# Four pre-LN graph layers on one core: kept blocks copied ahead of a row's weights, new planning numbers, and a new end

## The chip, the cores and the metric

One core of a Trainium2 chip runs the whole program. Five engines work side by side: TensorE (PE) multiplies, VectorE (DVE) and ScalarE (ACT) do elementwise work, GpSimd (POOL) does a little of both, and SyncE (SP) issues most of the transfers. The metric is the time of one launch on the device, in microseconds (us); the median of three runs is given.

## The reference

Sixteen graphs (batches) of 1,024 nodes with 128 features pass through four layers. Each layer adds its result to x; all of them use the same dense 1024 x 1024 adjacency `adj`, symmetric in its pattern, not in its values.

```python
h = relu(layernorm(x)); x = x + L0(h, adj)      # and so for L1, L2, L3
# L0: three times (relu after the first two)
h = h @ W + b
nh = h / max(norm(h), EPS)
h = (adj * (nh @ nh.T)) @ h
# L1
y = relu(((1 + eps) * h + adj.T @ h) @ W1 + b1) @ W2 + b2     # zero where masked
# L2: attention of one head
h = h @ W
attn = softmax(where(adj > 0, tanh(h @ a[:f] + (h @ a[f:]).T), -1e15))
y = where(sum(adj, 1) == 0, x, attn @ h)
# L3
h = x @ Ww.T + Wb
e = (h @ A) @ h.T;  e = e + e.T
att = softmax(where(adj > 0, e, 0), axis=1) * adj
hp = relu(att @ h)
i, f, o = sigmoid([x, hp] @ gate weights + biases)
y = o * tanh(sigmoid(i * hp + f * x))
```

## The kernel before

**Tiling.** A batch's x is one tile of 128 partitions by eight blocks of 128 columns: node 128c + p lies on partition p, block c. A 1024 x 1024 matrix is worked on in eight rows j of 128, each row in two halves s of 512 columns (four blocks). A half fills one PSUM bank.

**adj.** `turn` loads each row of the transposed adjacency in squares of 32 by 32, four transfers to a tile (L724, on SP), turns the squares on DVE (L732), and sums rows on ACT (L735). Batch b + 1's tiles are loaded while batch b runs.

**Layer 0.** Each of three sublayers (named 00, 01, 02) projects h (PE, L461), adds the bias and scales (L505 where the scale is the last sublayer's norm), flips h into hTn (PE transposes L451, ACT copies L483), sums squares on ACT and DVE (L770, L776), and raises them to −1/2 on GpSimd (`rn`, L444). Then for every row j: `square.row` fills the two halves of the row of h hT in PSUM (`sq`), `ew` on DVE multiplies it with rn and adj (L791), and PE accumulates with it (L671 or L682).

**The symmetric square.** h hT is symmetric, so `Square` multiplies only the blocks on and above the diagonal (L609). The blocks above the diagonal are kept in an SBUF tile `above`, and a later row transposes them back into its bank with PE (`mirrored`, L619). `keep` writes them: a copy on ACT (L641), behind L791 in the program, from the bank that L791 reads. A bank of PSUM is read by one engine after the other: the planner makes every operation on a bank wait for the one before it if that is on another engine. In batches 1 to 13 (`FAR`) the lower left quarter takes another way: DVE transposes rows 0 to 3's right halves (L631), SP sends them to HBM and fetches them back as squares (L651, L662), and DVE reads them in SBUF (`got`). Layer 3 uses the same class with e = g hT, where g is arranged to make it symmetric.

**Layers 1 to 3.** Layer 1 accumulates over adj rows loaded plainly (`adjL`) and runs two small matmuls (L471, L844). Layer 2 makes scores on ACT (tanh L906, exp L910), masks them on DVE (L914), and accumulates on PE (L682). Layer 3, for a row: mask (L973, reading the square's bank), row maximum (L984), exp on ACT (L988), times adj in two halves on DVE (L995), a scale of h's row by the sum (`hs`, L1004), accumulation (L671). Its end: hpT (L483), a projection `psN` (L461), hp (L1017), three gates for each node (add L1029, tanh L1035, scale L1038), z = hn * gate on GpSimd (L1043), z = hp * gate + z on DVE (eight instructions of 128 x 128, L505), two tanh on ACT (L1049, L1050), z = z * gate + x on DVE (again eight, L505), and the output's transfer (L1056, issued on ACT's queue).

**The order of work.** No engine chooses at run time: each works through its instructions as they were written. A list scheduler, `Plan`, writes them. Every operation has a planned duration, its predecessors and its buffers. At each step the planner takes the operations that could start next, and among those that can start within `WINDOW` of the earliest on the same engine it takes the one with the lowest rank: the batch's due time (`b * PERIOD`, and `(B - 2) * PERIOD + LAST` for the last), less the work behind it, less a lead from the table `LEADS` for this kind of operation (the key is layer, engine and buffer). `POOLS` gives how many buffers of a kind there are and `KINDS` how many a use may hold, with a smaller share for later batches. So work of up to three batches stands mixed in each engine's queue.

Of the kernel before, what the change touches and what calls it, by code (L numbers as in the profile page):

```python
# [53 lines left out]
class Plan:  # L54
# [53 lines left out]
    def link(self):  # L108

        for o in self.ops:
            for b in [b for b in o.new if b.kind == "ps"]:
                for r in b.users:
                    if r is not o:
                        for t in [t for t in r.new if t.kind not in self.psum]:
                            r.new.remove(t)
                            o.new.append(t)
        behind = {o: set(o.preds) for o in self.ops}
        for o in self.ops:  # L120
            for b in o.new:
                for u in b.users:
                    if u is not o:
                        self.place_after(u, o)
                        behind[u].add(o)
        for o in self.ops:
            for b in [b for b in o.new if b.kind in self.psum]:
                for u in b.users:
                    for p in behind[u]:
                        if p.seq < o.seq:  # L130
                            self.place_after(o, p)
        for o in reversed(self.ops):
            o.tail = o.us + max((s.tail + o.lat for s in o.succs), default=0.0)
            o.rank = (self.deadline(o.batch) - o.tail - self.leads.get(o.key, 0.0), o.seq)
# [87 lines left out]
def tile_adj_preln(  # L222
# [97 lines left out]
    for load_it in first:  # L320
# [11 lines left out]
    POOLS = {"adjT": 16, "adjL": 5, "x": 3, "big": 13, "above": 2, "got": 1, "bank": 8, "small": 24, "row": 5, "hbm": 3}  # L332
    KINDS = {
        "adjT": ("adjT", 16, 16), "adjL": ("adjL", 5, 5), "x": ("x", 3, 3), "w4": ("big", 9, 8),
        "chunk": ("big", 10, 4), "above": ("above", 2, 1), "got": ("got", 1, 1), "ps": ("bank", 4, 4),
        "acc": ("bank", 8, 5), "small": ("small", 16, 6), "row": ("row", 5, 5), "hbm": ("hbm", 3, 2),
    }
    PERIOD, LAST, AHEAD, WINDOW = 66.0, 23.0, 2, 0.05

    LEADS = {  # L340
        "0 ACT hT": 3.5, "0 ACT hn": 18.5, "0 DVE hn": 14.5, "0 DVE nb": -43.5, "0 DVE st": -4, "0 PE ps": 13.5,
        "0 POOL rstd": -24, "00 ACT above": 74, "00 ACT hTn": -86, "00 ACT params": -0.5, "00 ACT sq": 49,
        "00 DMA by": 16.5, "00 DMA got": 16.5, "00 DVE above": -7.5, "00 DVE ew": 1, "00 DVE h": -224.5,
        "00 DVE params": 64.5, "00 DVE ss": 12.5, "00 PE acc0": -62, "00 PE ps": 81.5, "00 PE psP": 523.5,
        "00 PE sq": -15, "00 POOL rn": -26.5, "01 ACT above": 69, "01 ACT hT": 19, "01 ACT hTn": -158,
        "01 ACT sq": 4.5, "01 DMA by": 18.5, "01 DMA got": 31, "01 DVE above": 1.5, "01 DVE ew": 316.5,
        "01 DVE h": 20, "01 PE ps": 12, "01 PE psP": 27, "01 PE sq": 55.5, "01 POOL rn": 19, "02 ACT above": -1,
        "02 ACT hTn": -32, "02 ACT sq": -30.5, "02 DMA by": 21, "02 DVE above": -1, "02 DVE ew": -53.5,
        "02 DVE h": 3, "02 DVE ss": -403, "02 DVE x": -30, "02 PE acc0": -29.5, "02 PE ps": -131.5,
        "02 PE psP": 13, "02 PE sq": -24.5, "02 POOL rn": 20, "1 DMA adjL": -497, "1 DVE adjL": 4.5,  # L350
        "1 DVE hn": 238, "1 DVE mv": 35.5, "1 DVE nb": -17, "1 DVE st": -449, "1 DVE x": -3.5,
        "1 PE acc1": -32.5, "1 PE py": -31.5, "1 PE py2": -32, "1 POOL rstd": -28, "2 ACT e2": -33.5,
        "2 ACT h": 2, "2 ACT hfl": -64, "2 ACT hn": -370, "2 ACT hnT": -5.5, "2 ACT s1": 1.5,
        "2 DVE alone": -36, "2 DVE e2": 5.5, "2 DVE h": -125.5, "2 DVE hn": 74.5, "2 DVE hrow": 5,
        "2 DVE mv": 60, "2 DVE nb": 263.5, "2 DVE rden": 23, "2 DVE st": 153, "2 DVE x": 18.5, "2 PE p1": -18,
        "2 PE pf": -240.5, "2 PE ps": -21, "2 PE psP": -186, "2 POOL rstd": -12.5, "3 ACT above": -206,
        "3 ACT e3": -111.5, "3 ACT gT": -84, "3 ACT gate": 81.5, "3 ACT h3T": -30.5, "3 ACT hn": -79,
        "3 ACT hnT": 243, "3 ACT hp": -80.5, "3 ACT hpT": 102.5, "3 ACT hs": -38.5, "3 ACT z": -290.5,
        "3 DMA by": 49, "3 DMA z": 1.5, "3 DVE e3": -89, "3 DVE gate": 68.5, "3 DVE h": -14.5, "3 DVE hn": 4.5,
        "3 DVE nb": -41, "3 DVE st": -5.5, "3 DVE sum": -15.5, "3 DVE z": -618, "3 PE acc3": -42.5,  # L360
        "3 PE pg": -27, "3 PE ps": 23, "3 PE psN": -301.5, "3 PE psP": -25, "3 PE sq": -17.5,
        "3 POOL rstd": -23.5, "3 POOL z": 3.5, "T DMA adjT": -143, "T DVE adjT": -223.5, "x DMA x": -51,
# [4 lines left out]
    def op(engine, us, reads, writes, fn, port=False, lat=None):  # L367
        o = plan.op(engine, us, reads, writes, fn, now[0], port, lat)
        t = (list(writes) + list(reads))[0]
        o.key = f"{now[1]} {engine} {(t[0] if isinstance(t, tuple) else t).name.split('_')[0]}"  # L370
        return o
# [4 lines left out]
    def act(us, reads, writes, fn):  # L376
        return op("ACT", us, reads, writes, fn)

    def dve(us, reads, writes, fn, port=False):
        return op("DVE", us, reads, writes, fn, port)  # L380
# [27 lines left out]
    FAR = range(1, B - 2)  # L408
# [37 lines left out]
    def flip(src, lo, hi, dst, w=D):  # L446
# [6 lines left out]
        pe((hi - lo) * TR, [blk(src, lo, hi, w)], [dst], emit)  # L453

# [59 lines left out]

    def layernorm(k, xt, behind=None):
# [47 lines left out]

        lo, hi = HALVES[0]
# [5 lines left out]
    def relu(t):  # L570

        lo, hi = HALVES[0]
# [120 lines left out]
    def load(b):  # L693
        xt = Buf("x", [P, N], f"x_{b}")
        op(
            "DMA", 2.2, [], [xt],
            lambda: nc.sync.dma_start(by_block(xt.t), x[b].rearrange("(c p) d -> p c d", p=P)),
        )
# [41 lines left out]
    def layer0(b, xt, aT, prepared):  # L740
        now[1] = "0"
        hn = layernorm(f"{b}_0", xt)
        hT = flipped(hn, f"hT_{b}_0", AF.Relu)
        rn = None
        for i in range(3):
# [18 lines left out]
            hTn = flipped(h, f"hTn_{k}")  # L764
            ss = small(f"ss_{k}", NB)
            sq = w4(f"sq_{k}")
            for lo, hi in HALVES:
# [15 lines left out]
            square = Square(k, hTn, hTn, b in FAR)  # L783
            acc = [bank(f"acc0_{k}_{s}") for s in range(2)]
            for j in range(NB):
                ew = chunk(f"ew_{k}_{j}")
                for s, (lo, hi) in enumerate(HALVES):
                    pc, view = square.row(j, s)
                    o = dve(
# [7 lines left out]
                    square.keep(j, s, pc)  # L797
# [15 lines left out]
    def layer1(b, xt, prepared):  # L813
# [6 lines left out]
        add_scaled(xt, D, 0, NB, b12, 0, 0, maskT, m, xt, True)  # L820
# [30 lines left out]
    def layer2(b, xt, aT, su):  # L851
# [10 lines left out]
        add_scaled(xt, D, 0, NB, hn, 0, D, alone, 0, xt, True)  # L862
# [25 lines left out]
        s1 = w4(f"s1_{b}")  # L888
        for s, (lo, hi) in enumerate(HALVES):
            p1 = ps(f"p1_{b}_{s}")  # L890
# [50 lines left out]
    def layer3(b, xt, aT):  # L941
# [3 lines left out]
        hnT = flipped(hn, f"hnT_{k}", AF.Relu)  # L945
        relu(hn)
        gT = w4(f"gT_{b}")
        for s, (lo, hi) in enumerate(HALVES):
            p = ps(f"pg_{b}_{s}")
            wide(p, wg, hnT, lo, hi)  # L950
            evict(p, gT, lo, hi, AF.Identity, bg)
# [12 lines left out]
        hT = flipped(h, f"h3T_{b}", w=E3)  # L964
        square = Square(k, gT, hT, b in FAR)
        acc = [bank(f"acc3_{b}_{s}") for s in range(2)]
        for j in range(NB):
            e = chunk(f"e3_{b}_{j}")
            for s, (lo, hi) in enumerate(HALVES):
                p, view = square.row(j, s)  # L970
                dve(
# [7 lines left out]
                square.keep(j, s, p)  # L979
# [12 lines left out]
            for lo, hi in HALVES:  # L992
# [29 lines left out]
        gate = small(f"gate_{b}", 3 * NB)  # L1022

        def of(g, n=NB):
            return gate.t.rearrange("p (g c) -> p g c", g=3)[:, g, :]

        dve(
            TINY, [hp, h], [gate],
            lambda: nc.vector.tensor_add(  # L1029
                gate.t.rearrange("p (g c) -> p c g", g=3),  # L1030
                by_block(hp.t, E3)[:, :, D:], by_block(h.t, E3)[:, :, D:],
            ),
            True,
        )
        act(0.22, [gate], [gate], lambda: nc.scalar.activation(gate.t, gate.t, AF.Tanh, scale=0.5))  # L1035
        dve(
            TINY, [gate], [gate],
            lambda: nc.vector.tensor_scalar(gate.t, gate.t, 0.5, 0.5, op0=ALU.mult, op1=ALU.add), True,  # L1038
        )
        z = w4(f"z_{b}")  # L1040
        pool_op(
            1.9, [hn, gate], [z],
            lambda: nc.gpsimd.tensor_mul(by_block(z.t), by_block(hn.t), per_node(of(1))),  # L1043
        )
        add_scaled(z, D, 0, NB, hp, 0, E3, gate, 0, z, True)

        def squash():
            v = z.t[:, 0:N]
            nc.scalar.activation(v, v, AF.Tanh, scale=0.5)  # L1049
            nc.scalar.activation(v, v, AF.Tanh, scale=0.5, bias=half)  # L1050

        act(S(N) + S(N, True), [z], [z], squash)
        add_scaled(z, D, 0, NB, z, 0, D, gate, 2 * NB, xt, True)
        op(
            "DMA", 2.0, [z], [],
            lambda: nc.scalar.dma_start(out[b].rearrange("(c p) d -> p c d", p=P), by_block(z.t)),  # L1056
        )
# [77 lines left out]
    with tc.manual_schedule():  # L1135
        for o in ordered:
            for t in o.new:
                src = psum if t.kind in plan.psum else hbm if t.kind == "hbm" else pool
# [36 lines left out]
```

## Time and profile before

| | us |
|---|---|
| median of three runs (2484.53 to 2487.31) | 2484.54 |
| the profiled execution | 2483.96 |
| its span, first to last instruction | 2481.8 |
| PE busy | 2410.6 |
| DVE busy | 2119.4 |
| ACT busy | 1287.1 |
| POOL busy | 214.4 |
| transfers | 263.35 MB, 106 GB/s |

A profile line for a group of instructions gives the kernel's line, engine, operation, the tiles written and read, the shapes and the count; then busy us and the mean ns of one; then the engine's idle time just before these instructions, with what ended most of it. In a list of instructions the columns are start, length, and then the same; square brackets hold the idle time before and its releaser. A list of stretches gives the length, the busy time of each engine with the instructions in brackets, the granted TensorE clock (1.00 is full), the share of time in which the transfer engines worked, and GB/s. Matmul ends are modelled, so the spacing of starts says more than busy time.

### The profile page before, as it was taken

To read this page: it belongs to the slowest core of one execution; us is meant where nothing else is said; L and a number is where in the kernel's file an instruction comes from. 1 tells how busy PE (TensorE), PEld (TensorE's weight loads), DVE (VectorE), ACT (ScalarE), POOL (GpSimd) and SP (SyncE) were. 2 spreads that over 40 slices of the span, in tenths; PEclk is the share of its full clock that TensorE was granted. 3 is DMA by queue.
4 is the path that set the end of the run, shared out by engine and by line. 5 is a ranking of instruction groups with operands and counts; after the bars stand their busy time and mean duration, and the time that the engine had idled before them with its cause. 6 is when DMAs were issued, how large, how long until landed. Compare 5 with 4: busy or idle time off the path is not lost.

```text
span 2481.8 us, 34726 instructions
## 1 busy us (share of the span) xinstructions
PE 2410.6 (97%) x11946; PEld 1588.7 (64%) x11946; DVE 2119.4 (85%) x5278; ACT 1287.1 (52%) x2401; POOL 214.4 (9%) x134
## 2 busy tenths in 40 slices
PE   6999999999999999999999999999999999999987
PEld 3567566675766657566675766756566575765763
DVE  6767989898897989889898897988989899796777
ACT  4425554644646455454554636456454655554575
POOL 1000010010101011011010100101011010010100
PEclk9999999999999999999999999999999999999998
DMA  7622827648284563936648276473945638054100
GB/s 125 129 67 69 163 59 143 138 80 167 60 160 121 99 140 84 165 91 127 129 94 178 52 154 135 84 154 68 165 107 111 136 85 162 1 108 80 35 1 18
DMA packets 1129441, 263.35 MB, mean 106 GB/s; under 512 B 971824, under 2 KB 1112880, under 8 KB 1129264
## 3 DMA queue, kind: packets, MB, share of 16 engines
q1 hardware_dynamic: 1108352, 251.73, 50.0%
q10 hardware_dynamic: 20912, 9.40, 1.4%
q8 instruction: 94, 1.54, 0.3%
q14 instruction: 83, 0.68, 0.1%
HBM read 198.14 MB, written 62.91 MB: 105 GB/s over the span
## 4 chain that ended last, share of the span: by engine, by line
PE 78%; DVE 9%; ACT 7%; issue 2%; DMA 1%; SPq 1%; ACTq 0%; POOL 0%; POOLq 0%; DVEq 0%
PE acc L671 31%; PE sq L609 17%; PE acc L682 11%; PE psP L461 6%; PE sq L619 4%; ACT e L906 3%; DVE ew L791 3%; ACT e L910 3%; PE py L844 2%; PE py L471 2%; DVE e L914 2%; PE ps_hTn L451 1%; DVE z L505 1%; PE pg L471 1%; PE ps_hnT L451 1%
## 5 line engine op out<-in xcount | busy, mean ns | idle before, releaser
L791 DVE SCALAR_TENSOR_TENSOR ew<-sq,rn,adjT 128x512 f32<-128x512 f32 x612 | 436.9, 739 | 68.2 <-PE sq L619 32.0
L671 PE MATMUL acc<-ew,h 128*128 128x512 f32 x1024 | 480.6, 597 | 4.7 <-DVE ew L791 4.5
L609 PE MATMUL sq<-hTn 128*128 128x512 f32 (+3 forms) x1152 | 441.3, 489 | 0.4 <-ACT hTn L483 0.4
L641 ACT COPY above<-sq 128x384 f32<-128x384 f32 (+3 forms) x432 | 169.2, 394 | 403.9 <-DVE ew L791 366.5
L671 PEld LDWEIGHTS acc<-ew,h 128*128 128x128 f32 x1024 | 178.9, 191 | 174.0 <-issue 112.9
L609 PEld LDWEIGHTS sq<-hTn 128*128 128x128 f32 x1152 | 193.5, 191 | 124.0 <-issue 76.1
L682 PEld LDWEIGHTS acc<-h,e 128*128 128x128 f32 x2048 | 241.0, 192 | 29.3 <-DVE e L914 11.8
L682 PEld LDWEIGHTS acc<-h,ew 128*128 128x128 f32 x2048 | 240.8, 192 | 21.0 <-DVE ew L791 11.4
L444 POOL TENSOR_TENSOR rstd<-ve,mhalf 128x8 f32<-128x8 f32 x64 | 104.8, 1637 | 1725.7 <-DVE ve L536 1694.9
L682 PE MATMUL acc<-h,ew 128*128 128x128 f32 x2048 | 252.7, 276 | 0.4 <-DVE ew L791 0.4
L682 PE MATMUL acc<-h,e 128*128 128x129 f32 x2048 | 249.5, 277 | 2.8 <-DVE e L914 1.5
L671 PE MATMUL acc<-e,hs 128*128 128x512 f32 x512 | 240.6, 595 | 1.7 <-DVE e L995 1.7
L671 PE MATMUL acc<-adjL,hn 128*128 128x512 f32 x512 | 239.0, 595 | 0.1
L988 ACT ACTIVATE e<-e,top 128x1024 f32<-128x1024 f32 x128 | 147.1, 1149 | 173.0 <-DVE top L984 172.5
L735 ACT ACTIVATE adjT<-adjT 128x1024 f32<-128x1024 f32 x128 | 135.0, 1055 | 194.0 <-DVE adjT L732 163.7
L619 PEld LDWEIGHTS sq<-ident,above 128*128 128x128 f32 x960 | 125.7, 141 | 142.2 <-issue 74.0
L619 PE MATMUL sq<-ident,above 128*128 128x128 f32 x960 | 174.4, 275 | 27.8 <-ACT above L641 27.8
L914 DVE SCALAR_TENSOR_TENSOR e<-adjT,e 128x512 f32<-128x512 f32 x256 | 162.0, 683 | 41.9 <-ACT e L910 41.9
L732 DVE STREAM_TRANSPOSE adjT<-adjT 128x1024 f32<-128x1024 f32 x128 | 155.2, 1225 | 17.8 <-DMA adjT<-in_adj_dram 10.9
L995 DVE TENSOR_TENSOR e<-e,adjT 128x512 f32<-128x512 f32 x256 | 166.2, 680 | 0.0
L906 ACT ACTIVATE e<-s,h 128x1024 f32<-128x1024 f32 x128 | 143.1, 1141 | 38.4 <-issue 36.6
L631 DVE STREAM_TRANSPOSE above<-sq 128x512 f32<-128x512 f32 x208 | 147.0, 707 | 10.5 <-PE sq L609 9.1
(124 smaller groups left out, 3455.9 us busy)
## 6 DMA issues: line engine op xcount, KB each, us to landing
adjT<-in_adj_dram SPq DMA_DIRECT2D x512, 128.0 KB, 3.7
adjL<-in_adj_dram SPq DMA_DIRECT2D x128, 512.0 KB, 4.9
by_hbm<-above SPq DMA_DIRECT2D x104, 512.0 KB, 3.2
got<-by_hbm SPq DMA_DIRECT2D x416, 128.0 KB, 3.0
x<-in_x_dram SPq DMA_DIRECT2D x16, 512.0 KB, 5.3
out_dram<-z ACTq DMA_DIRECT2D x16, 512.0 KB, 3.3
b<-in_L_gnn_b_dram ACTq DMA_DIRECT2D x4, 64.0 KB, 3.8
w<-in_L_gnn_W_dram ACTq DMA_DIRECT2D x2, 128.0 KB, 3.8
```

The lines of the kernel that those rows point to most:

```text
L461: nc.tensor.matmul(dst.t[:, (c - lo) * n : (c - lo + 1) * n], cols(srcT.t, c), w, start=True, stop=True)
L609: lambda: nc.tensor.matmul(dst.t[:, (first - lo) * P :], cols(leftT.t, j), span(rightT.t, first, hi), start=True, stop=True),
L619: nc.tensor.transpose(cols(dst.t, r), cols(above.t, p), ident)
L641: lambda: nc.scalar.copy(span(above.t, p, p + hi - first), read.t[:, (first - lo) * P :]),
L671: lambda s=s, lo=lo, hi=hi: nc.tensor.matmul(acc[s].t, cols(h.t, at, w), span(ew.t, lo, hi), start=(j == 0), stop=(j == NB - 1)),
L682: nc.tensor.matmul(a.t[:, (c - lo) * n : (c - lo + 1) * n], cols(ew.t, c), h.t[:, j * w : j * w + n], start=(j == 0 and c == lo), stop=(j ...
L732: dve(V(N), [t], [t], lambda t=t: nc.vector.transpose(t.t, t.t), True)
L791: lambda view=view, ew=ew, rn=rn, j=j, lo=lo, hi=hi: nc.vector.scalar_tensor_tensor(by_block(span(ew.t, lo, hi), D, 4), view(), rn.t[:, j ...
L906: lambda e=e, j=j: nc.scalar.activation(e.t[:, 0:N], s1.t[:, 0:N], AF.Tanh, bias=h.t[:, j * E2 + D + 1 : j * E2 + D + 2]),
L914: lambda e=e, j=j, lo=lo, hi=hi: nc.vector.scalar_tensor_tensor(span(e.t, lo, hi), span(aT[j].t, lo, hi), 0.0, span(e.t, lo, hi), op0=ALU. ...
L988: lambda e=e, top=top, tot=tot: nc.scalar.activation(e.t[:, 0:N], e.t[:, 0:N], AF.Exp, bias=top.t, accum_out=tot.t),
L995: lambda e=e, j=j, lo=lo, hi=hi: nc.vector.tensor_mul(span(e.t, lo, hi), span(e.t, lo, hi), span(aT[j].t, lo, hi)),
```

## The change

Five things are changed in the program, each under a letter in a set `FLAGS`; other letters of the set keep what the kernel had, and branches of letters not in the set issue nothing.

- **k**: `square.keep` stands ahead of the operation that weights a half row (L791 and L973), so ACT's copy of kept blocks, or DVE's transposition of them, is written before the weight on the same bank.
- **x**: batch 0's x is loaded by two transfers of half its blocks.
- **z**: in the last two batches, the odd rows of layer 3 are multiplied with adj on GpSimd, in one instruction of 128 x 1024, in place of two on DVE (L995).
- **y**: in the last two batches, z = hp * gate + z and z = z * gate + x are each a multiplication and an addition on GpSimd, in place of eight instructions on DVE (L505).
- **h**: the last batch's end, from the gates to the output's transfer, is done for four blocks and then for the other four. For this the gates of one node lie side by side (c g) where they were by kind (g c).

The planner gets other numbers: ACT's operations 0.03 us longer, DVE's 0.015; own leads for the first two and last two batches (keys that end in <0, <1, >1, >0), some 400 of them; all other leads new; PERIOD, LAST, and the limits on buffers new. What order it then writes follows from all of these.

```diff
-            o.rank = (self.deadline(o.batch) - o.tail - self.leads.get(o.key, 0.0), o.seq)
+            lead = self.leads.get(o.key + o.edge, self.leads.get(o.key, 0.0))
+            o.rank = (self.deadline(o.batch) - o.tail - lead, o.seq)
...
-    POOLS = {"adjT": 16, "adjL": 5, "x": 3, "big": 13, "above": 2, "got": 1, "bank": 8, "small": 24, "row": 5, "hbm": 3}
+    POOLS = {"adjT": 16, "adjL": 5, "x": 3, "big": 13, "above": 2, "got": 1, "bank": 8, "small": 29, "row": 8, "hbm": 3, "hrow": 2}
     KINDS = {
-        "adjT": ("adjT", 16, 16), "adjL": ("adjL", 5, 5), "x": ("x", 3, 3), "w4": ("big", 9, 8),
-        "chunk": ("big", 10, 4), "above": ("above", 2, 1), "got": ("got", 1, 1), "ps": ("bank", 4, 4),
-        "acc": ("bank", 8, 5), "small": ("small", 16, 6), "row": ("row", 5, 5), "hbm": ("hbm", 3, 2),
+        "adjT": ("adjT", 16, 16), "adjL": ("adjL", 5, 5), "x": ("x", 3, 3), "w4": ("big", 10, 6),
+        "chunk": ("big", 12, 4), "above": ("above", 2, 1), "got": ("got", 1, 1), "ps": ("bank", 8, 8),
+        "acc": ("bank", 8, 8), "small": ("small", 7, 6), "row": ("row", 4, 2), "hbm": ("hbm", 3, 2),
+        "hrow": ("hrow", 2, 1),
     }
-    PERIOD, LAST, AHEAD, WINDOW = 66.0, 23.0, 2, 0.05
+    PERIOD, LAST, AHEAD, WINDOW = 60.0, 9.0, 2, 0.05
...
+        o.edge = f" <{now[0]}" if now[0] < 2 else f" >{B - 1 - now[0]}" if now[0] > B - 3 else ""
...
-        return op("ACT", us, reads, writes, fn)
+        return op("ACT", us + 0.03, reads, writes, fn)
...
-        return op("DVE", us, reads, writes, fn, port)
+        return op("DVE", us + 0.015, reads, writes, fn, port)
...
-    FAR = range(1, B - 2)
+    FLAGS = set("Cabcdkxhyz")
+
+    LO, HI = 1, 2
...
+        for lo, hi in HALVES if "x" in FLAGS and b == 0 else ((0, NB),):
+            op(
+                "DMA", 2.2 * (hi - lo) / NB, [], [blk(xt, lo, hi)],
...
-            square = Square(k, hTn, hTn, b in FAR)
+            square = Square(k, hTn, hTn, "abc"[i] in FLAGS and LO <= b < B - HI)
...
                     pc, view = square.row(j, s)
+                    if "k" in FLAGS:
+                        square.keep(j, s, pc)
                     o = dve(
                         V(HALF, True), [pc, rn, blk(aT[j], lo, hi)], [blk(ew, lo, hi)],
...
-                    square.keep(j, s, pc)
+                    if "k" not in FLAGS:
+                        square.keep(j, s, pc)
...
-            for lo, hi in HALVES:
+            if ("5" in FLAGS or "z" in FLAGS and b >= B - 2) and j % 2:
+                pool_op(1.96, [e, aT[j]], [e], lambda e=e, j=j: nc.gpsimd.tensor_mul(e.t[:, 0:N], e.t[:, 0:N], aT[j].t))
+            for lo, hi in () if ("5" in FLAGS or "z" in FLAGS and b >= B - 2) and j % 2 else HALVES:
...
+            def scaled(a, w, g, c):
+
+                if "P" in FLAGS or ("y" in FLAGS and late):
+                    us = 0.2 + 1.7 * n / NB
+                    pool_op(us, [blk(a, lo, hi, w), at], [blk(a, lo, hi, w)], lambda: nc.gpsimd.tensor_mul(part(a, w), part(a, w), per_node(of(g), n)))
+                    pool_op(us, [blk(a, lo, hi, w), blk(c, lo, hi)], [blk(z, lo, hi)], lambda: nc.gpsimd.tensor_add(part(z), part(a, w), part(c)))
+                    return
...
+            scaled(hp, E3, 0, z)
+            act(S(n * P) + S(n * P, True), [blk(z, lo, hi)], [blk(z, lo, hi)], squash)
+            scaled(z, D, 2, xt)
...
+        for lo, hi in HALVES if "h" in FLAGS and b == B - 1 else ((0, NB),):
+            finish(lo, hi)
```

## The prediction

> **What bounds the kernel now.** I read the page's first two parts, then the costliest groups, then stretches of the span, then the instructions inside the worst stretch.
>
> ```profile
> PE 2410.6 (97%) x11946; PEld 1588.7 (64%) x11946; DVE 2119.4 (85%) x5278; ACT 1287.1 (52%) x2401; POOL 214.4 (9%) x134
> ...
> PEclk9999999999999999999999999999999999999998
> ...
> L641 ACT COPY above<-sq 128x384 f32<-128x384 f32 (+3 forms) x432 | 169.2, 394 | 403.9 <-DVE ew L791 366.5
> ...
> L619 PE MATMUL sq<-ident,above 128*128 128x128 f32 x960 | 174.4, 275 | 27.8 <-ACT above L641 27.8
> ```
>
> TensorE is the bound, at full clock, so only its gaps can be won. The copies L641 stand 366.5 us behind L791, but TensorE waits only 27.8 us for them (L619): the large number is idle time of an engine busy 52%. Stretches (columns: length, then busy us of PE, PEld, DVE, ACT, POOL; clock; DMA share; GB/s), first two steady batches, cut where the chain of waits repeats, then the first 62 us and the last 124:
>
> ```profile
> 637.20:787.27 150.07, 148.26 (x736) 97.60 (x735) 133.71 (x333) 78.79 (x148) 13.35 (x8) 1.00 0.57 120
> 787.27:937.30 150.03, 148.24 (x736) 97.62 (x735) 133.78 (x333) 78.79 (x148) 13.35 (x8) 1.00 0.59 120
> ...
> 0.00:62.00 62.00, 42.79 (x154) 24.60 (x155) 37.43 (x104) 25.34 (x50) 8.93 (x11) 0.92 0.79 125
> ...
> 2357.90:2419.90 62.00, 55.49 (x320) 40.42 (x319) 46.24 (x131) 44.01 (x78) 3.27 (x2) 0.95 0.00 1
> 2419.90:2482.00 62.10, 44.07 (x167) 24.57 (x165) 49.25 (x104) 33.49 (x66) 3.79 (x2) 0.86 0.06 18
> ```
>
> A steady batch takes 150.05 us. Busy time overstates what TensorE must do, since matmuls overlap; from start to start within back-to-back runs one takes 429 ns (128x512), 112 ns (128x128), 109 ns (a transpose). One batch's 734 matmuls come to 146.5 us that way, so 3.5 us per batch are gaps. One of them is 1.86 us, in layer 2's end, where the next batch's second sublayer starts:
>
> ```profile
> 502.23 1.02 PE L609 MATMUL sq<-hTn 128*128 128x512 f32 x2
> ...
> 504.30 1.42 DVE L791 SCALAR_TENSOR_TENSOR ew<-got,rn,adjT 128x512 f32<-128x512 f32 x2
> ...
> 505.64 0.74 DVE L791 SCALAR_TENSOR_TENSOR ew<-sq,rn,adjT 128x512 f32<-128x512 f32 x1
> ...
> 506.41 0.48 ACT L641 COPY above<-sq 128x384 f32<-128x384 f32 x1 [6.14 <-DVE ew L791]
> ...
> 506.94 0.33 PE L619 MATMUL sq<-ident,above 128*128 128x128 f32 x1 [1.70 <-ACT above L641]
> ```
>
> The square is done by 503.2, ACT has been idle for 6.14 us, but the copy is written behind the weight on the same bank, and that weight is behind statistics and two other weights on DVE. The other gaps are about a dozen of 0.1 to 0.3 us.
>
> **The change, part by part.** Sums are made against the profiled execution, 2483.96 us (span 2481.8 and 2.2 around it); the median, 2484.54, is 0.6 above.
>
> *Copies ahead of weights.* ACT's copy (0.26 to 0.58 us) needs the square alone. In the new order 1.39 us of matmul work lie between the tightest square and its mirrored blocks; 0.48 of copy fit, with 0.03 and 0.05 us of signalling before and after it in the rows above and 0.3 allowed for the square's own tail, so the 1.86 us go: −1.9 per batch. The price: each L791/L973 weight on such a row waits 0.3 to 0.6 us longer, because a bank is read by one engine after the other. DVE is busy 133.7 of 150.05 us, so a late weight is not always hidden: in the rows after 507 weights reach the accumulating matmuls with 1.1 to 1.5 us to spare. For batches 1 to 13, on rows 0 to 3, the work ahead of the weight is DVE's own 0.71 us transposition (L631), which puts that weight and its matmuls back by 0.71 us but the HBM round trip forward by as much; SP's queue issues the same transfers.
>
> *New order from the new leads, limits and durations.* The plan's numbers issue nothing themselves, and the gates' new layout keeps its instructions (0.20, 0.22 and 0.18 us on the tail). The matmuls are the same 6,968 forms in another order. In the second sublayer's opening the last batch's eight L505 rows (2.17 us of DVE) now stand between the two reductions, and its two tanh (2.2 us of ACT) ahead of a copy: I estimate a new gap of 0.75 us. Weights late behind copies I estimate at 0.1 to 0.3. So the gaps go from 3.5 to about 2.5 us: −1.0 to −1.1 per batch, over 12 batches −13. Bounds: all but 1.2 us of gaps gone, −28; the new waits eat the gain and half as much again, +6.
>
> *Batch 0's x in halves.* One issue more on SP, whose queue sets the start: batch 0's 32 adjT issues run from 1.9 to 47.8 us, 1.44 us each; a contiguous half costs about 0.5 us (x's own issue). The first statistics can begin a half transfer sooner, but the first sublayer's last rows stay tied to adjT, whose last square lands at 51.5 us. Together with copies no longer waited for at 46.6 and 53.9 us (0.83 and 1.75 us idle before L619): −2, between −5 and +1.
>
> *End, DVE's side.* In the last 124 us DVE sets the pace from 2410 on (9.47 busy of 10.3 us at 2413.8 to 2424.1). Each of the eight odd rows of the last two batches gives 2 x 0.68 us of L995 to GpSimd, and batches 14 and 15 give 2 x 2.17 us of L505 each. Of this 2.2 to 4.5 us lie ahead of the last row's maximum; ACT loses about 2.6 us of batch-14 work ahead of the last layer-2 exponentials; against it the last row's product takes 1.90 instead of 1.36. The last accumulation, now ended at 2462.7, comes 6.5 us sooner, between 1 and 10. Here the clock matters: after waits of 2.0 and 2.2 us for copies it stood at 0.50 from 2413.8 to 2424.1. The Trainium skill ("TensorE: Matmul & The Clock Gate", the table of the clock gate's states) has half speed only after an idle window of about 3.4 us, ended by as much work. By the rule those waits cost no clock and nothing is won; by the row the matmuls in it lost about 3 us, but beside a full DVE. I take 1 us of it, inside the 6.5.
>
> *End, GpSimd's side.* After the last matmul everything is a chain:
>
> ```profile
> 2462.68 0.60 ACT L483 ACTIVATE hpT<-acc 128x512 f32<-128x512 f32 x1 [3.00 <-PE acc L671]
> ...
> 2468.78 1.90 POOL L1043 TENSOR_TENSOR z<-hn,gate 128x1024 f32<-128x1024 f32 x1 [11.36 <-DVE gate L1038]
> 2470.71 2.19 DVE L505 SCALAR_TENSOR_TENSOR z<-hp,gate,z 128x128 f32<-128x128 f32 x8 [2.07 <-POOL z L1043]
> ...
> 2475.26 2.19 DVE L505 SCALAR_TENSOR_TENSOR z<-z,gate,x 128x128 f32<-128x128 f32 x8 [2.36 <-ACT z L1050]
> 2477.52 0.38 ACTq L1056 DMA_DIRECT2D out_dram<-z  x1
> ```
>
> It takes 19.1 us to 2481.8, 4.3 of them from the last issue. In the new order batch 14's gate needs a projection that stands behind the last accumulation on PE, so both batches' ends fall here, and with L505 moved to GpSimd they stand in one queue: five operations of 128x1024 at 1.90 and ten of 128x512 at about 1.0 (half a row), 19.5 to 20.5 us. It begins about 2.5 us after the last matmul, and the last output issue follows it: 2.5 + 20 + 4.3 = 27, 8 us longer than now. The rule that speaks against this part is the skill's ("GPSIMD Engine Reference", Performance versus the Vector engine): about 2.6 cycles an element where VectorE has one, which makes 2.2 us of 1,024 (estimate) and a queue of 22; the row with 1.90 is this operation itself, and I take it. The end as a whole: 8 − 6.5 = +1.5, between −3 and +8.
>
> **Sum.** −2 − 13 + 1.5 = −13.5 on 2483.96 gives 2470.5; with the median's 0.6, 2471.
>
> **The rivals.** (1) *Deeper gain*: the new order also closes most of the dozen small gaps and the opening's new gap doesn't come; gaps 1.2 us a batch, −28, with start and end −3: 2453. For it: ACT has 48% idle time and every copy can go at once. Against: DVE at 89% leaves weights little room. (2) *A wait for another*: weights behind copies stop the accumulating matmuls as often as copies stopped the mirrored ones; gaps stay 3.5, start −2, end +1.5: 2484, no change. For it: the small slack named above. (3) *GpSimd's tail decides*: the queue of 20 us stands, the last accumulation isn't sooner, because GpSimd's 1.90 us products on odd rows hold up the last rows, +8; with gaps at 3.5 and the start's −2 that is 2491, slower. With the end at +8 it is slower at all once the middle wins under 6 us, and by more than 0.2% under 1. For it: fifteen operations in one queue; against it: the middle's 1.86 us wait has an idle engine behind it in every batch.
>
> **How the numbers follow.** 0.2% (5 us) is about what a measurement of this kernel tells from no change. Chances: forecast 0.47, deeper gain 0.26, a wait for another 0.14, GpSimd's tail 0.13. The forecast with its neighbours (2462 to 2478) is faster, as is the deeper gain: 0.73 faster, 0.14 the same, 0.13 slower. The range runs from 2450 (rival 1 and its start) to 2488 (rival 2 and part of 3).
>
> **What would show it.** Right: L641's idle time behind L791 falls from 366.5 to a few tens; the wait of L619 for L641 from 27.8 to under 8; a steady batch from 150.05 to about 149; fifteen GpSimd rows end to end after the last accumulation, the span ending about 27 us behind it. Wrong: a steady batch at 150 or above with waits of L671 for L791 beyond 10 us in all, a last accumulation later than 2450, or a start whose first 62 us do more than 3 us of matmul work more or less.

## The result and the profile after

The changed kernel takes 2463.64 us (median of four runs, 2461.61 to 2464.46) where the kernel before takes 2484.53 beside it: a ratio of 0.9913, 95% interval 0.9895 to 0.993. Run once more in a later series it gave 0.990 (0.9885 to 0.9915). That is 20.9 us less; 13.5 were forecast (2471, range 2450 to 2488).

The profiled execution took 2464.46 us, its span 2462.7. The page's first two parts, and the rows of the kept copies and the mirrored blocks (L785 and L763 are L641 and L619 of before):

```profile
PE 2397.5 (97%) x11946; PEld 1592.9 (65%) x11946; DVE 2106.1 (86%) x5232; ACT 1291.5 (52%) x2404; POOL 254.5 (10%) x155
...
PEclk9999999999999999999999999999999999999998
...
L785 ACT COPY above<-sq 128x384 f32<-128x384 f32 (+3 forms) x432 | 167.6, 392 | 431.8 <-PE sq L763 257.4
...
L763 PE MATMUL sq<-ident,above 128*128 128x128 f32 x960 | 175.5, 274 | 5.5 <-ACT above L785 5.4
```

ACT still stands idle for long before its copies, but now until their own square is there and not until a weight on VectorE is done, and TensorE waits 5.4 us for them where it was 27.8. The list of waits says what has come in its place (us in total, times, longest):

```profile
DVE ew L952 <- ACT above L785: 33.0, 44, 1.8
...
PE acc L815 <- DVE ew L952: 8.3, 9, 2.4
...
PE acc L826 <- DVE ew L952: 0.9, 2, 0.6
```

Weights do wait for copies, 33 us in layer 0 (and 5.4 in layer 3), but little of it can reach TensorE: its accumulations wait 9.2 us for weights in all, 7.0 of them in the first batch. Two steady batches and the end as stretches (length; busy PE, PEld, DVE, ACT, POOL; clock; DMA share; GB/s):

```profile
1055.80:1203.60 147.80, 147.45 (x735) 97.72 (x735) 133.84 (x333) 79.03 (x147) 13.32 (x8) 1.00 0.64 121
1352.30:1500.10 147.80, 147.45 (x735) 97.82 (x735) 133.75 (x334) 79.03 (x147) 13.79 (x8) 1.00 0.65 122
...
2401.30:2462.70 61.40, 35.73 (x134) 19.67 (x132) 31.55 (x52) 28.02 (x57) 31.81 (x20) 0.81 0.06 18
```

The engines do the same work in a steady batch (VectorE 133.8 us, as before); these two batches are 147.8 us long (those from the fourth batch's layer 2 to the fourteenth's, 147.3 to 148.8) where it was 150.05. In the last 61 us GpSimd is busy for 31.8, as much as VectorE.

**The span, taken apart.** The matmuls are the same, and each shape has a usual distance from one start to the next (429, 112, 109 ns; 2366.3 us for all of them). What a stretch takes beyond these distances is called gaps here; the slower matmuls at half clock count in it too. The two spans, one profile each, cut at layer 2's small projection (L884, after it L1057) of each batch, come out as:

| us | before | after | difference | forecast |
|---|---|---|---|---|
| until the first matmul | 10.3 | 11.9 | +1.6 | |
| gaps, up to the first batch's layer 2 | 25.5 | 18.4 | −7.1 | |
| gaps, up to the second's | 4.0 | 5.1 | +1.1 | start in all −2 |
| gaps, twelve batches | 42.2 | 17.4 | −24.8 | −13 |
| gaps, from the fourteenth batch's layer 2 to the last matmul | 18.6 | 17.6 | −1.0 | |
| from the last matmul's start | 15.0 | 25.9 | +10.9 | end in all +1.5 |
| span, with 2366.3 of matmuls | 2481.8 | 2462.7 | −19.2 | −13.5 |

A second profile of the changed kernel (the later series) has 16.7 us of gaps in the twelve batches, 16.4 from the fourteenth on and the same 25.9 at last, so a difference of a microsecond in a row of this table says nothing. The total is near the forecast because two of its terms missed in opposite directions: the middle won twice as much, and the end lost 10 us instead of 1.5, outside its bounds of −3 to +8. That they nearly cancel is luck. Both traces have the same 11,946 matmuls in the same shapes; the prediction's 6,968 stands in neither. The experiments went to the middle and the end.

### The profile page after: what moved, and what is told of

Its sections match the earlier page's. It is cut to its first block, busy times and chain, and to the rows that moved or that the text cites. A ratio compares the mean times of both kernels' runs of the same rounds, so it can differ in the third digit from the quotient of the medians.

```text
span 2462.7 us, 34845 instructions
## 1 busy us (share of the span) xinstructions
PE 2397.5 (97%) x11946; PEld 1592.9 (65%) x11946; DVE 2106.1 (86%) x5232; ACT 1291.5 (52%) x2404; POOL 254.5 (10%) x155
## 4 chain that ended last, share of the span: by engine, by line
PE 86%; DVE 5%; DMA 4%; ACT 3%; SPq 1%; POOL 1%; issue 0%; POOLq 0%; DVEq 0%; ACTq 0%
PE acc L815 33%; PE sq L753 17%; PE acc L826 17%; PE psP L593 6%; PE sq L763 4%; PE py L1014 2%; PE py L603 2%; PE ps_hTn L562 2%; DMA adjT<-in_adj_dram 1%; DMA by_hbm<-above 1%; PE ps_hnT L562 1%; PE pg L603 1%; DVE ew L952 1%; PE psN L593 1%; SPq L872 1%; DMA got<-by_hbm 1%
## 5 line engine op out<-in xcount | busy, mean ns | idle before, releaser
L815 PE MATMUL acc<-ew,h 128*128 128x512 f32 x1024 | 488.0, 598 | 8.6 <-DVE ew L952 8.3
L753 PE MATMUL sq<-hTn 128*128 128x512 f32 (+3 forms) x1152 | 432.3, 488 | 0.4 <-ACT hTn L615 0.3
L785 ACT COPY above<-sq 128x384 f32<-128x384 f32 (+3 forms) x432 | 167.6, 392 | 431.8 <-PE sq L763 257.4
L753 PEld LDWEIGHTS sq<-hTn 128*128 128x128 f32 x1152 | 198.8, 191 | 152.6 <-issue 104.3
L826 PE MATMUL acc<-h,e 128*128 128x129 f32 x2048 | 243.1, 277 | 3.4 <-DVE e L1102 3.4
L815 PE MATMUL acc<-adjL,hn 128*128 128x512 f32 x512 | 229.6, 593 | 0.1
L763 PEld LDWEIGHTS sq<-ident,above 128*128 128x128 f32 x960 | 125.2, 141 | 122.1 <-issue 79.2
L763 PE MATMUL sq<-ident,above 128*128 128x128 f32 x960 | 175.5, 274 | 5.5 <-ACT above L785 5.4
L1102 DVE SCALAR_TENSOR_TENSOR e<-adjT,e 128x512 f32<-128x512 f32 x256 | 161.5, 685 | 14.6 <-ACT e L1098 14.4
L775 DVE STREAM_TRANSPOSE above<-sq 128x512 f32<-128x512 f32 x208 | 147.3, 709 | 21.6 <-PE sq L753 19.6
L815 PEld LDWEIGHTS acc<-adjL,hn 128*128 128x128 f32 x512 | 93.9, 190 | 102.8 <-issue 88.1
L1194 DVE TENSOR_TENSOR e<-e,adjT 128x512 f32<-128x512 f32 x240 | 157.2, 686 | 0.0
```

The lines of the kernel that those rows point to most:

```text
L753: lambda: nc.tensor.matmul(dst.t[:, (first - lo) * P :], cols(leftT.t, j), span(rightT.t, first, hi), start=True, stop=True),
L763: nc.tensor.transpose(cols(dst.t, r), cols(above.t, p), ident)
L775: lambda: nc.vector.transpose(span(above.t, p, p + 4), read.t),
L785: lambda: nc.scalar.copy(span(above.t, p, p + hi - first), read.t[:, (first - lo) * P :]),
L815: lambda s=s, lo=lo, hi=hi: nc.tensor.matmul(acc[s].t, cols(h.t, at, w), span(ew.t, lo, hi), start=(j == 0), stop=(j == NB - 1)),
L826: nc.tensor.matmul(a.t[:, (c - lo) * n : (c - lo + 1) * n], cols(ew.t, c), h.t[:, j * w : j * w + n], start=(j == 0 and c == lo), stop=(j ...
```

## The experiments

**Copies ahead, in the order before.** Is it the copies' place that closes the gaps, or the new order? The four combinations tell. The first takes the kernel before and only moves each of ACT's copies in front of its weight, after the planner is done; VectorE's transpositions stay where they were.

```diff
     ordered = plan.order()
+    ahead = {o: c for o, c in early if c is not None}     # weight: its copy
+    moved = set(ahead.values())
+    ordered = [x for o in ordered if o not in moved for x in (([ahead[o]] if o in ahead else []) + [o])]
```

> The kernel before, every queue in the order it had, except that each of ACT's copies L641 stands directly ahead of its weight (L791 or L973) in place of behind it; DVE's transpositions L631 stay where they were. If the copies' place is what the middle gained by: the 1.86 us gap goes from twelve batches and the waits at 46.6 and 53.9 us from the start, -24, some 2460 us, a steady batch at 148.2. If the new order and its leads did it and the moved copy only makes the weights late: within 5 us of 2484, a steady batch at 149.7 or more, with L671's waits for L791 taking the place of L619's for L641.

Measured: 2525.59 us, ratio 1.0153 (1.0138 to 1.0168). Neither theory had this: slower by 38 us. Its waits, and a steady batch as a stretch:

```profile
DVE ew L791 <- ACT above L641: 95.6, 132, 2.2
...
PE acc L682 <- DVE ew L791: 17.3, 21, 1.3
...
PE acc L671 <- DVE ew L791: 15.5, 31, 3.7
...
PE sq L619 <- ACT above L641: 2.5, 2, 1.3
```

```profile
635.50:786.90 151.40, 149.37 (x737) 97.51 (x736) 133.82 (x333) 78.73 (x148) 13.36 (x8) 1.00 0.56 119
```

TensorE's wait for copies is gone (2.5 us), as the mechanism says. But the weights wait 95.6 us for copies, and accumulating matmuls wait 32.8 us for weights, where the kernel before had some 5. A steady batch has 4.85 us of gaps where it had 3.5: the 1.86 us went and 3.2 came. The largest is 1.2 us in one piece, for a weight in the third sublayer; four more are 0.34 to 0.44, two of them for weights. The other part of the loss lies in the transitions: 11.9 us of gaps in the second batch (4.0 before) and 33.8 from the fourteenth on (18.6).

**Copies behind, in the new order.** The opposite combination: the changed kernel's order, in which each copy is put behind its weight after planning, or just ahead of the mirrored blocks where these come first.

```diff
     ordered = plan.order()
+    for weight, copy in early:
+        if copy is None:
+            continue
+        i, w = ordered.index(copy), ordered.index(weight)
+        end = next(n for n in range(i + 1, len(ordered)) if ordered[n] is not weight and ordered[n] in copy.succs)
+        ordered.insert(min(w + 1, end), copy)
+        del ordered[i]
```

> The changed kernel in the order it has, but each of ACT's copies L785 that can stand directly behind its weight does so (some 370 of 432); where the mirrored blocks come before the weight, the copy stands just ahead of them. If the copies' place and the new order need each other: waits of L763 for L785 return, the gaps of a steady batch go from 1.6 to 3 us or more, +17 us or more on the changed kernel. If the new order alone closes the gaps: within 5 us of the changed kernel.

Measured: 2526.36 us, 1.0152 (1.0135 to 1.0169), 63 us above the changed kernel, which took 2463.13 us beside it:

> The changed kernel once more, as the neighbour of the runs beside it: 0.991 of the kernel before, 2463 us where before is 2484.5.

The list of waits of the run with the copies behind:

```profile
PE sq L763 <- ACT above L785: 56.2, 69, 7.3
...
PE acc L815 <- DVE ew L951: 4.7, 5, 2.1
```

The wait is the old one, L763 for L785, and larger than ever. Twelve batches have 62 us of gaps.

| gaps of twelve batches (total time) | copies behind weights | copies ahead |
|---|---|---|
| order before | 42.2 (2484.5) | 60.8 (2525.6) |
| new order | 62.0 (2526.4) | 17.4 (2463.6) |

The times are of three series, in which the kernel before took 2484.5, 2487.5 and 2488.3 us. In these two orders neither part wins anything without the other; each alone costs 1.5%. The new order is one that gives the weights time, and only early copies fit it. Not run: the planner with the copies ahead and the old leads, which might have found an order of its own for them.

**Parts of the plan alone.** Three runs let the planner write the whole order anew with one thing of the change taken out.

```diff
-    FLAGS = set("Cabcdkxhyz")
+    FLAGS = set("Cabcdxhyz")
```

> The changed kernel with the copies behind their weights again, planned with its own new leads, durations and limits. If the copies' place did the middle: a steady batch back at 150 or above, +20 or more on the changed kernel, 2484 to 2490 us. If the new leads did it: a steady batch stays under 149, 2464 to 2470 us.

Measured: 2775.14 us, 1.1156. The direction is the first theory's, but more than ten times its size, and so it says little of the copies: twelve batches hold 291 us of gaps, with TensorE 13 us at a stretch waiting for a weight in layer 0's third sublayer. The new leads, which came together with the copies ahead, write a bad order without them.

```diff
-        o.edge = f" <{now[0]}" if now[0] < 2 else f" >{B - 1 - now[0]}" if now[0] > B - 3 else ""
+        o.edge = ""
```

> The changed kernel planned with the new general leads alone, without the own leads of the first two and last two batches. If those leads made the start's 7 us: the gaps up to the second batch's layer 2 go from 18.4 back to 25 us or more, and the end's from 14.8 up, 2475 to 2490 us, while the middle's batches stay at 148. If they do nothing: within 3 us of the changed kernel.

Measured: 2612.88 us, 1.0499, far beyond what either theory had. From the sixth batch's layer 2 to the fourteenth's the gaps are 1.3 to 1.5 us a batch, as in the best batches of the changed kernel: the steady order doesn't need the own leads. All the loss is in the transitions: the first matmul at 24.6 us instead of 11.9, 48 us of gaps in the first two batches instead of 24, then 34, 31, 22 and 5 us, and 49 at the end instead of 18. After a start that doesn't fit, the steady order is reached only four batches later.

```diff
-        return op("ACT", us + 0.03, reads, writes, fn)
+        return op("ACT", us, reads, writes, fn)
...
-        return op("DVE", us + 0.015, reads, writes, fn, port)
+        return op("DVE", us, reads, writes, fn, port)
```

> The changed kernel planned with ACT's and VectorE's operations as long as before (0.03 and 0.015 us shorter), all leads as changed. If the leads fit the planned durations that they were chosen with, as they proved to fit the copies' place: tens of us slower, 2480 to 2600 us. If the durations matter little: within 5 us of the changed kernel.

Measured: 2642.79 us, 1.062, the first theory's direction and above its range. 183 us of gaps in twelve batches, uneven from 1 to 37 us a batch. Whether longer durations are better in themselves can't be read from this, since the leads belong to them; it was not tried with leads chosen anew.

**x in one transfer.** In the changed kernel's own order, the first half's step loads all of x and the second's nothing.

```diff
-                lambda lo=lo, hi=hi: nc.sync.dma_start(
-                    by_block(span(xt.t, lo, hi), D, hi - lo),
-                    x[b].rearrange("(c p) d -> p c d", p=P)[:, lo:hi],
-                ),
+                (lambda: None) if 0 < lo else lambda: nc.sync.dma_start(
+                    by_block(xt.t), x[b].rearrange("(c p) d -> p c d", p=P)
+                ),
```

> The changed kernel in its own order, but batch 0's x comes in one transfer, at the place of the first half's. The first statistics of the second half started at 6.87 us in the changed kernel, where a whole x let them start at 5.22. If the halves cost the start: first matmul 1 to 2 us sooner than 11.9 us, and, where it is not lost to adjT's squares later, up to 2 us on the whole. If adjT's squares set the first batch's pace: the first matmul sooner, and the end of that batch, and the total, within 1 us of the changed kernel.

Measured: 2462.27 us, 0.9896 (0.9881 to 0.991), the changed kernel within the noise. The first statistics of each kernel (changed first, then this run):

```profile
4.03 0.87 DVE L663 BATCH_NORM_STATS2 st<-x 128x6 f32<-128x128 f32 x4 [3.12 <-DMA x<-in_x_dram]
6.87 0.87 DVE L663 BATCH_NORM_STATS2 st<-x 128x6 f32<-128x128 f32 x4 [1.97 <-DMA x<-in_x_dram]
```

```profile
5.28 1.65 DVE L663 BATCH_NORM_STATS2 st<-x 128x6 f32<-128x128 f32 x8 [4.37 <-DMA x<-in_x_dram]
```

The first half starts 1.2 us sooner, the second 1.6 later, and the normalization needs both: the first matmul is at 11.86 with halves, at 10.80 without. It makes no difference, because the first batch waits for adjT later: at 51.3 us TensorE stands 4.00 us for a weight in the run with whole x, 2.38 us at 52.1 in the changed kernel. The halves are worth nothing here. The start's gain needs the own leads (without them the start was worse than before the change); which of them makes it was not tried.

**The end: GpSimd's queue.** In the changed kernel's own order, the last two batches' z = a * gate + c is emitted as eight VectorE instructions where the order has the addition; where it has the multiplication, nothing.

```diff
-                    pool_op(us, [blk(a, lo, hi, w), at], [blk(a, lo, hi, w)], lambda: nc.gpsimd.tensor_mul(part(a, w), part(a, w), per_node(of(g), n)))
-                    pool_op(us, [blk(a, lo, hi, w), blk(c, lo, hi)], [blk(z, lo, hi)], lambda: nc.gpsimd.tensor_add(part(z), part(a, w), part(c)))
+                    pool_op(us, [blk(a, lo, hi, w), at], [blk(a, lo, hi, w)], lambda: None)
+                    pool_op(us, [blk(a, lo, hi, w), blk(c, lo, hi)], [blk(z, lo, hi)], eight)   # eight: L505's loop, on VectorE
```

> The changed kernel in its own order, but where the last two batches' z = a * gate + c is two operations on GpSimd, it is eight on VectorE at the same place of the order. If the queue of fifteen operations on GpSimd sets the end: 28.7 us from the last accumulation to the end become about 19, as before the change, so -9 to -11, some 2454 us. If the end is held by the gates and tanh behind the last accumulation and not by that queue: within 3 us of 2464.

Measured: 2456.41 us, 0.9877 (0.9862 to 0.9891), and from the last accumulation's first copy (hpT) to the end 20.5 us instead of 28.7. This is the changed kernel's tail that it shortens; every row on GpSimd follows the one before:

```profile
2433.97 0.60 ACT L615 ACTIVATE hpT<-acc 128x512 f32<-128x512 f32 x1 [2.06 <-PE acc L815]
...
2436.91 1.91 POOL L1248 TENSOR_TENSOR hp<-hp,gate 128x1024 f32<-128x1024 f32 x1 [4.15 <-DVE gate L1262]
...
2438.77 1.92 POOL L1265 TENSOR_TENSOR z<-hn,gate 128x1024 f32<-128x1024 f32 x1
...
2440.77 2.16 POOL L1249 TENSOR_TENSOR z<-hp,z 128x1024 f32<-128x1024 f32 x1
...
2454.09 1.90 POOL L1248 TENSOR_TENSOR z<-z,gate 128x1024 f32<-128x1024 f32 x1
2456.07 2.34 POOL L1249 TENSOR_TENSOR z<-z,x 128x1024 f32<-128x1024 f32 x1
```

The queue runs from 2436.91 to 2458.41, 21.5 us, and the last output needs 4.3 more. The last accumulation itself was no later for having these rows on VectorE. From batch 15's small projection in layer 2 (L1057) to the accumulation's first copy it took 80.8 us in this run; the two profiles of the changed kernel have 82.1 and 80.9. Moving these rows off VectorE had not made it sooner.

**The end: odd rows.** Again in the changed kernel's own order, the eight products of the last two batches' odd rows as two VectorE halves each.

```diff
-                pool_op(1.96, [e, aT[j]], [e], lambda e=e, j=j: nc.gpsimd.tensor_mul(e.t[:, 0:N], e.t[:, 0:N], aT[j].t))
+                def halves(e=e, j=j):
+                    for lo, hi in HALVES:
+                        nc.vector.tensor_mul(span(e.t, lo, hi), span(e.t, lo, hi), span(aT[j].t, lo, hi))
+
+                pool_op(1.96, [e, aT[j]], [e], halves)
```

> The changed kernel in its own order, but the odd rows of layer 3 of the last two batches are multiplied with adj in two halves on VectorE, where the order has GpSimd's one. As the prediction had it (VectorE sets the pace of the last 60 us and is relieved): the last accumulation comes 4 to 6 us later, 2469 us. If GpSimd's product, which took 2.35 to 2.73 us there and not 1.90, gave back what it took off VectorE: within 2 us of 2464. If it costs more than it saves: 2458 to 2462.

Measured: 2466.45 us, 0.9914 (0.9898 to 0.9931). The ratio can't be told from the changed kernel's; the traces say more. The last accumulation's copy is at 2437.76, 3.8 us later, but 1.75 of these were lost before any of the eight products, as the last batch's small projection shows (the changed kernel's, then this run's):

```profile
2351.90 0.39 PE L1057 MATMUL pf<-w2f,hrow 128*128 128x128 f32 x2
```

```profile
2353.64 0.39 PE L1057 MATMUL pf<-w2f,hrow 128*128 128x128 f32 x2
```

From there to the copy it takes 84.1 us, where the changed kernel's two profiles have 82.1 and 80.9; the tail behind it is the same. So this part wins 2.0 to 3.3 us, less than the 4 to 6 expected. GpSimd's product takes 2.51 us on average and not 1.90:

```profile
L1190 POOL TENSOR_TENSOR e<-e,adjT 128x1024 f32<-128x1024 f32 x8 | 20.1, 2515 | 56.9 <-ACT e L1185 56.2 <-PE sq L763 0.7
```

**The end: batch 14's gate.** Beyond VectorE for z, the last 53 steps of the order are permuted by hand: batch 14's last projection, copy and gates go ahead of batch 15's last accumulation, and its products between batch 15's gates and products.

```diff
     ordered = plan.order()
+    end = ordered[-140:]
+    ordered[-53:] = [end[n] for n in (
+        87, 88, 89, 101, 90, 91, 92, 93, 94, 95, 96, 104, 106, 108, 111, 97, 98, 99, 113, 115, 100, 102, 103, 107, 105, 110, 109,
+        112, 114, 117, 116, 119, 120, 121, 123, 124, 118, 122, 125, 126, 127, 129, 128, 131, 136, 138, 139, 130, 132, 134, 133, 135, 137,
+    )]      # 101, 104, 106, 108, 111: batch 14's last projection, copy, gates; 97 to 99: batch 15's last accumulation
```

> As the run with z = a * gate + c on VectorE, and of the last 53 steps of the order batch 14's end is moved forward: its last projection, copy and gates stand ahead of batch 15's last accumulation, its products between batch 15's gates and products. If batch 14's gate behind the last accumulation is what the rest of the tail waits for: the end comes 3 to 5 us sooner than in that run, 2450 to 2453 us. If the tail is batch 15's own chain of gate, GpSimd, VectorE, ACT and VectorE: within 1.5 us of that run's 2455.

Measured: 2454.28 us, 0.9863 (0.9848 to 0.9878), beside the changed kernel's 2463.13. From hpT's first copy to the end it is 18.2 us, 2.3 us less than in the run before this edit, while the same stretch repeats within 0.15 us over five profiles of runs with GpSimd's tail. The first theory had 3 to 5; the median lies 1.3 us above its range and inside the second theory's. So batch 14's gate was a small part of the tail. In the rest batch 14's products still stand between batch 15's on VectorE.

**The end: two engines side by side.** One of the eight products goes back to VectorE, the one beside batch 15's last normalization.

```diff
+                    if (b, j) != (B - 2, 3):
+                        return nc.gpsimd.tensor_mul(e.t[:, 0:N], e.t[:, 0:N], aT[j].t)
+                    for lo, hi in HALVES:
+                        nc.vector.tensor_mul(span(e.t, lo, hi), span(e.t, lo, hi), span(aT[j].t, lo, hi))
```

> As the run with the end's order moved, but of the eight products on GpSimd one, batch 14's row 3, is two on VectorE again, at its place in the order: GpSimd's stood beside four normalizations on VectorE (L691) that took 3.15 us for 1.1. If the two engines lock each other out there: L691 is back at 1.1 us, the 3.1 us wait of PE ahead of hnT's transposes shrinks by 1 us or more, and the last accumulation comes 0.5 to 2 us sooner, 2452 to 2454 us. If VectorE's own queue is what makes it late: the 1.36 us product delays it, and the end is 0 to 2 us later.

Measured: 2453.29 us, 0.986 (0.9844 to 0.9877). The four instructions in the changed kernel, GpSimd's product beside them, and then the four in this run:

```profile
2386.25 3.15 DVE L691 TENSOR_SCALAR hn<-x,mv,rstd 128x128 f32<-128x128 f32 x4
...
2386.41 2.38 POOL L1190 TENSOR_TENSOR e<-e,adjT 128x1024 f32<-128x1024 f32 x1 [0.70 <-PE sq L763]
```

```profile
2384.52 1.11 DVE L691 TENSOR_SCALAR hn<-x,mv,rstd 128x128 f32<-128x128 f32 x4
```

L691 is back at 1.1 us, and TensorE's gap ahead of hnT's transposes goes from 3.10 to 2.27. The gaps from the last batch's layer 2 on go from 14.4 to 12.8 us, but the changed kernel's two profiles differ there by 1.2 already; in the medians it is 1 us, less than their intervals. The place is shown, the gain in total is not. This version is the fastest of all, 34.7 us under the kernel before beside it. The end in two halves of four blocks (h) was not run alone.

## Why the prediction was right, and where it was not

*The wait for copies.* Right in place, in cause and in size: L619's 27.8 us are 5.4, and the steady gap of 1.86 us is gone. The new gap in the second sublayer's opening came too, for the reason given: the copy stands behind the last batch's two tanh on ACT. In the batch below, the second of them runs from 1063.65 for 1.15 us, and the copy follows at 1064.70. The gap is 0.51 us beyond the usual distance where 0.75 was estimated:

```profile
1065.22 0.33 PE L763 MATMUL sq<-ident,above 128*128 128x128 f32 x1 [0.35 <-ACT above L785]
```

*Weights behind copies, "0.1 to 0.3" a batch.* Right for the order that was built (2 us of TensorE's waits for weights behind the first batch, in the whole trace), but for a reason that the prediction didn't have. It argued that the slack of 1.1 to 1.5 us would hide a copy's 0.3 to 0.6. The order before has that slack and loses 3.2 us a batch. The cover for this cost is the new order, not the slack; had the copies been moved alone, the forecast of a gain would have been wrong by its sign.

*The middle, −13: the term that was too small.* It kept the other gaps at about 1.9 us less the first. Measured is 1.3 in half of the batches and 1.45 on average, of which 0.51 is the new one: the dozen small gaps, 1.6 us together, fell to some 0.9. Gone are those ahead of layer 2's accumulations (0.8 us) and of the third sublayer's (0.3). The order was read for the one large wait and its distance to the mirrored blocks; that it also spaces weights and accumulations better was left at "as before". What came true in the middle is rival 1 (1.2 us a batch), which was given a chance of 0.26.

*The start, −2.* −4.4, within its bounds, but not by the halves of x, which bring nothing. Of the two waits for copies at 46.6 and 53.9 us, one of 1.08 us is left (at 41.4), and new waits for weights stand beside it.

*The end, "6.5 us sooner": the step that failed.* The odd rows on GpSimd did relieve VectorE, by 2.0 to 3.3 us; of the z rows nothing is seen; 2.2 to 4.5 were claimed for both. But the last accumulation is 28.7 us sooner than before, and the start and the middle already make −29.2: nothing is left. In the table, the end's gaps ahead of the last matmul fell by 1.0 us. The new order has other waits there: 3.6 us beyond the usual distance ahead of batch 15's accumulation in layer 2, and 1.7 and 3.1 around its last normalization. The idle times in brackets are a little shorter:

```profile
2358.93 0.80 PE L826 MATMUL acc<-h,e 128*128 128x129 f32 x2 [3.42 <-DVE e L1102]
...
2385.71 0.49 PE L753 MATMUL sq<-h3T,gT 128*128 128x128 f32 x2 [1.56 <-DVE e L1169]
...
2391.23 1.14 PE L562 MATMUL ps_hnT<-ident,hn 128*128 128x128 f32 x5 [2.94 <-DVE e L1169]
```

The half clock came with them, from 2357.7 to 2364.5 and from 2391.8 to 2395.3: 10.2 us together, as long as at the end of the kernel before. I had removed the old waits from the sum and put no new ones in.

*The tail, 27 us.* Measured 28.7, from GpSimd's queue as described: 21.5 us where 20 were summed. Multiplications kept to 1.90 us, additions took 2.16 and 2.34. The rule that was weighed against the row, 2.2 us for 1,024 elements, made 22 and was nearer in sum, and the additions' 2.16 and 2.34 lie about it; the single row was right for the operation that it showed and not for its neighbour. Rival 3 had the tail's place right; it didn't decide, because the middle won far more than the 6 us under which the whole would have been slower.

## What to carry to other kernels

A step put ahead of another on the same bank moves a wait, it doesn't remove one: it pays only where the order of the work behind it is made for it, so price the pair, and test both alone. Leads belong to the program and the planned durations that they came with: changing either by a little (0.015 and 0.03 us, one flag) cost 7 to 13% against the changed kernel. An engine that is free in the steady state isn't free at the end: before moving the last steps to it, add up its queue after the last matmul.

## What the runs showed of the hardware that was not expected

VectorE can stand still for as long as a row on GpSimd lasts. Beside GpSimd's product, four normalizations took 3.15 us for 1.11, and nearly all of the difference is in one of them, 2.38 us for 0.34; with the product taken away (the last experiment) it was gone. Of each pair of small gate instructions in these lines the first took 1.70 and 1.60 us, the second 0.16, and the first ended as GpSimd's row did:

```profile
2437.14 1.79 DVE L1237 TENSOR_TENSOR gate<-hp,h 128x12 f32<-128x12 f32 x2 [0.37 <-ACT hp L1216]
...
2439.12 1.68 DVE L1262 TENSOR_SCALAR gate<-gate 128x12 f32<-128x12 f32 x2 [0.20 <-ACT gate L1261]
```

VectorE's products that read PSUM (L1169, 0.68 us) kept their time. This agrees with the Trainium skill's "SBUF — State Buffer", on who interferes with whom, which has the two engines share a pair of ports that one of them holds for a whole instruction; the sizes are this trace's.

GpSimd itself loses less by it. Its product of two SBUF tiles took 2.35 to 2.38 us four times, once with VectorE idle but for the first 0.1 us:

```profile
2430.41 2.35 POOL L1190 TENSOR_TENSOR e<-e,adjT 128x1024 f32<-128x1024 f32 x1 [2.88 <-ACT e L1185]
```

```profile
2430.36 0.17 DVE L1199 RECIPROCAL sum<-sum 128x1 f32<-128x1 f32 x1
```

The other four took 2.61 to 2.73, and each of these began while VectorE was in an operation on two SBUF tiles (L1102 or L1194). So what sets the 2.35 apart from the 1.90 of a multiplication by the gates isn't VectorE; the second operand, a full tile, is likely, as the additions show, but no run tests it.

The clock fell to 0.50 at 43.5 us in the changed kernel as well, after a wait of TensorE of 1.08 us and within the next, of 1.65, and stayed there to 50.3:

```profile
43.47:50.30 6.83, 5.49 (x6) 1.85 (x6) 2.92 (x7) 1.42 (x3) 1.64 (x1) 0.50 0.55 92
```

As in the kernel before, shorter waits than the rule's 3.4 us, which the prediction weighed, were enough. All thirteen traces together show what they have in common. Every stretch at half clock ahead of the last matmul begins on one grid of 3.41 us and lasts one to five of its steps (10.24 us is three, 6.83 two). Counted by the usual distances at full clock, the matmuls in the step before each of the 109 falls came to 1.26 us or less, and in every step at full clock that no fall followed, from the clock's first record on, to 1.26 or more. So here it is not one long wait that costs the clock, but less than some 37% of matmul work in one step.
